# A masked attention kernel with 536 instead of 544 token places in its short path

## Chip, cores and metric

One core of one Trainium2 chip runs the whole program. The metric is the device time of one execution in microseconds. Everything is float32.

## The reference, cut to what matters

Eight sequences (B = 8) of T = 1024 tokens with D = 512 features go through one attention layer with eight heads and a residual. Queries, keys and values are the same projection `q`. The mask holds 0 or 1 for each token.

```python
def _L0_cond_ref(x, mask, Wq, Wo):          # x: (8, 512, 1024)
    xt = jnp.transpose(x, (0, 2, 1))
    q = xt @ Wq.T
    qh = q.reshape(B, T, NH, dk).transpose(0, 2, 1, 3)     # NH = 8, dk = 64
    scores = scale * jnp.einsum('bhqd,bhkd->bhqk', qh, qh)
    cmask = mask[:, None, None, :]
    rmask = mask[:, None, :, None]
    logits = (scores * cmask + (1.0 - cmask) * NEG) * rmask
    attn = jax.nn.softmax(logits, axis=-1)
    ctx = jnp.einsum('bhqk,bhkd->bhqd', attn, qh)
    out = ctx.transpose(0, 2, 1, 3).reshape(B, T, D) @ Wo.T
    return jnp.transpose(out, (0, 2, 1))
x = x + _L0_cond_ref(x, cond_2048, Wq, Wo)
```

A masked key gets weight zero. A masked query has all its logits at zero, so its attention is the plain mean over all 1024 tokens. Both follow from the mask alone: only the kept tokens (mask 1) need scores, and all masked queries of a batch share one context, the mean. The mask is drawn with a chance of 0.5063 for each token, so about half of the tokens are kept.

## The kernel before

The kernel packs the kept tokens of each batch into a fixed number of places NK, and the last place, NK - 1, stands for the mean. `early` (L1008) ranks the tokens of all masks, and a value that the program reads, the largest number of kept tokens in any batch (with 2T times over 1 added if a mask isn't 0 or 1), chooses a path at L1438 to L1445: `late(SHORT)` below 544, `late(LONG)` below 576, and otherwise a kernel over all tokens. `fit_to(n)` (L330) sets NK = n, KH = n / 2 and END = n - 512. Places are handled in NC = 5 chunks: four of 128 (LP = 512 places) and a last one of END, 32 in the path before.

A *pair* is two heads of one batch, that is 128 features; there are 32 pairs, four for each batch, taken in order. The loop at L1324 runs each pair through five steps c = 0 to 4. At each step TensorE gets, in a hand-written order:

- `scores(pair, c)` (L651): the scores of chunk c against all NK places, in two halves of KH columns, for two heads and two half chunks, as 64x64 matmuls on the four quarters of the array (L662; L676 for the last chunk). ScalarE turns them into exponentials (L685).
- at c = 0 and 1 `project` (L529) of the next pair: 64x64 matmuls over KH columns, the upper half with one more column for the mean (L542). `take_queries` (L554) then copies the two halves into `qT` (L558 on ScalarE, L559 on VectorE), fills `qT` behind place NK up to W = 640 places with copies of the last END columns (L560), and keeps the mean (L565).
- `weigh` (L697): values times exponentials, KH columns each, 64x64 again (L709).
- at c = 2 `turn_values` (L567): 64x64 transposes of the next pair's `qT` to `v` (L579, L588); then squares, lengths and biases for it.
- between them, by the plan of `plan` (L1179), work for other batches: gathering kept tokens (`gather`, L467, on POOL's queue), transposing them into `xc` (`collect`, L480), output products of finished batches (`output`, L822, whose results POOL's queue stores to `od` in DRAM at L846), `fetch` (L942: rows of `od` gathered and added to rows of x, also on POOL's queue), and `finish_blocks` (L909: VectorE transposes of finished rows into `whole`, stored by SP's queue).

`invert` (L779) sends the reciprocal sums through DRAM and back by SP's queue (`row`, `rb`); `contexts` (L808) multiplies them into the context `cT`, and copies the mean into its last column (L812). For the last batch `begin_output` and `end_output` (L856, L872) make the output product in two parts, and `fetch_last` and `finish_tokens` finish it.

Each engine's queue runs in order. So on VectorE the copies of `qT` stand behind whatever was put before them, `finish_blocks` and `contexts` included.

The output product of the last chunk is only END tokens wide. `output` therefore lays `parts = 128 // END` pieces of the 512 features side by side on the 128 partitions, and stores each with a DMA of its own.

Of the kernel before, what the change touches and what calls it, by code (L numbers as in the profile page):

```python
# [10 lines left out]
F32 = mybir.dt.float32  # L11
I32 = mybir.dt.int32
AF = mybir.ActivationFunctionType
ALU = mybir.AluOpType
# [5 lines left out]
NEG = -1e30  # L20
BIG = 3.0e38
Q = 32
SHORT = 544
LONG = 576
TINY = 1e-26

# [279 lines left out]
def attention_of_kept_tokens(ctx, tc, x, mask, wq, wo, out, ident, wqT, woT, verdict, flag):  # L306


    nc = tc.nc
    B, D, T = x.shape  # L310
    P = 128
    DK = D // NH
    SCALE = 1.0 / math.sqrt(DK)
    ND = D // P
# [8 lines left out]
    LP = LAST * P  # L323
    W = NC * P
    assert LP < SHORT < LONG == LP + DK and DK == P // 2
    NK = KH = END = 0
    sizes, places = [], []
    heads = [slice(h * DK, (h + 1) * DK) for h in range(2)]

    def fit_to(n):  # L330
        nonlocal NK, KH, END
        NK, KH, END = n, n // 2, n - LP
        assert DK % END == 0
        sizes[:] = [P] * LAST + [END]
        places[:] = [slice(END + c * P, END + (c + 1) * P) for c in range(LAST)] + [slice(0, END)]

    sb = ctx.enter_context(tc.tile_pool(name="fsb", bufs=2))
# [23 lines left out]
    def bank(name, tag="t"):  # L361
        return ps.tile([P, NB], F32, tag=tag, name=name, bufs=2)
# [141 lines left out]
    qTs, qms, vs, tops, biases, shares = {}, {}, {}, {}, {}, {}  # L504
# [2 lines left out]

    def place_queries(pair):
        b, pr = pair
        qTs[pair] = sb.tile([P, W], F32, tag="qT", name=f"qT_{b}_{pr}", bufs=2)  # L510
        pqs[pair] = [bank(f"pq_{b}_{pr}_{hf}") for hf in range(2)]

    def project_first(pair):

        b, pr = pair
        place_queries(pair)
        for hf in range(2):
            n = KH + hf
            for d in range(ND):
                nc.tensor.matmul(  # L520
                    pqs[pair][hf][:, :n],
                    wqT[:, d, pr * P : (pr + 1) * P],
                    xcs[b][:, d, hf * KH : hf * KH + n],
                    start=(d == 0),
                    stop=(d == ND - 1),
                )
        take_queries(pair)

    def project(pair, cross):  # L529


        b, pr = pair
        if not cross:
            place_queries(pair)
        for d in range(ND):
            for r in range(2):
                rows = slice(r * DK, (r + 1) * DK)
                hf = r ^ cross
                n = KH + hf
                for h in range(2):  # L540
                    at = pr * P + h * DK
                    mm = nc.tensor.matmul(  # L542
                        pqs[pair][hf][heads[h], :n],
                        wqT[rows, d, at : at + DK],
                        xcs[b][rows, d, hf * KH : hf * KH + n],
                        start=(not cross and d == 0),
                        stop=(cross == 1 and d == ND - 1),
                    )
                    if cross:
                        pass_gate(mm)  # L550
        if cross:
            take_queries(pair)

    def take_queries(pair):  # L554
        b, pr = pair
        qT = qTs[pair]
        lo, hi = pqs.pop(pair)
        note(nc.scalar.copy(qT[:, :KH], lo[:, :KH]))  # L558
        nc.vector.tensor_copy(qT[:, KH:NK], hi[:, :KH])  # L559
        nc.vector.tensor_copy(  # L560
            qT[:, NK:W].rearrange("p (r k) -> p r k", k=END),
            hi[:, KH - END : KH].unsqueeze(1).to_broadcast([P, (W - NK) // END, END]),
        )
        qms[pair] = sb.tile([P, 1], F32, tag="qm", name=f"qm_{b}_{pr}", bufs=4)
        nc.vector.tensor_copy(qms[pair], hi[:, KH : KH + 1])  # L565
# [68 lines left out]
    es, rbs, cTs, avs, begun = {}, {}, {}, {}, set()  # L634
# [3 lines left out]
    def note(read):  # L638
        reader[0] = reader[0] or read.ins.name
# [89 lines left out]
        weigh(pair, c - 1, cross)  # L729

    def place_contexts(pair):
        cTs[pair] = sb.tile([P, NK], F32, tag="cT", name="cT_%d_%d" % pair, bufs=2 * ND)
        return cTs[pair]

    def end_values(pair):
        cT = place_contexts(pair)
        for hf, av in enumerate(avs.pop(pair)):
            read = nc.scalar.copy(cT[:, hf * KH : (hf + 1) * KH], av[:, :KH])  # L738
        note(read)

    def end_values_last(pair):

        cT = place_contexts(pair)
        for hf, av in enumerate(avs.pop(pair)):
            cols = slice(hf * KH, (hf + 1) * KH)
            nc.vector.tensor_tensor(cT[:, cols], av[:, :KH], rbs[pair][:, cols], ALU.mult)
        nc.vector.tensor_copy(cT[:, NK - 1 : NK], qms.pop(pair))

    def spread(pair, inv):

# [48 lines left out]
    def sum_last(pair):  # L799

        rb = rbs[pair]
        end = rb[:, LP : LP + DK]
        nc.vector.tensor_tensor(end, end, rb[:, LP + DK : W], ALU.add)
        nc.vector.tensor_tensor(lowest, lowest, end, ALU.min)
        nc.vector.tensor_scalar(end, end, TINY, None, ALU.max)
        nc.vector.reciprocal(end, end)

    def contexts(pair):  # L808
        sum_last(pair)
        cT, rb = cTs[pair], rbs.pop(pair)  # L810
        nc.vector.tensor_tensor(cT, cT, rb[:, :NK], ALU.mult)
        nc.vector.tensor_copy(cT[:, NK - 1 : NK], qms.pop(pair))  # L812


    ods, gs, wholes, pos = {}, {}, {}, {}
# [1 line left out]
    def place_outputs(b):  # L817
        if b not in ods:
            ods[b] = dr.tile([NK, D], F32, tag="od", name=f"od_{b}")
        return ods[b]  # L820

    def output(b, i, k, of=2):  # L822

        n = sizes[i]
        parts = P // n
        w = D // parts
        if k == 0:
            pos[b, i] = sb.tile([P, D], F32, tag="oc", name=f"oc_{b}_{i}", bufs=NC)
        oc = pos[b, i]
        cols = slice(k * w // of, (k + 1) * w // of)  # L830
        po = bank(f"po_{b}_{i}_{k}")
        for pr in range(ND):
            for j in range(parts):
                nc.tensor.matmul(  # L834
                    po[j * n : (j + 1) * n, cols],
                    cTs[b, pr][:, i * P : i * P + n],
                    woT[:, pr, j * w + cols.start : j * w + cols.stop],
                    start=(pr == 0),
                    stop=(pr == ND - 1),
                )  # L840
        note(nc.scalar.copy(oc[:, cols], po[:, cols]))  # L841
        if k + 1 < of:
            return
        od = place_outputs(b)
        for j in range(parts):
            nc.gpsimd.dma_start(od[places[i], j * w : (j + 1) * w], oc[j * n : (j + 1) * n, :w])  # L846

    partials = {}

    def plain(pr):  # L850
        return woT[:, pr, :].rearrange("p (a d f) -> p d a f", a=A, d=ND)

    def as_plain(t):
        return t.rearrange("p (d a f) -> p d a f", a=A, d=ND)

    def begin_output(b, i):  # L856

        n = sizes[i]
        po = bank(f"pa_{b}_{i}")
        for pr in range(ND - 1):  # L860
            nc.tensor.matmul(  # L861
                as_plain(po[:n, :]),
                cTs[b, pr][:, i * P : i * P + n],
                plain(pr),
                start=(pr == 0),
                stop=(pr == ND - 2),
            )
        pa = sb.tile([P, D], F32, tag="xin", name=f"pa_{b}_{i}", bufs=NC)
        note(nc.scalar.copy(pa[:n, :], po[:n, :]))
        partials[i] = pa  # L870

    def end_output(b, i, tag):  # L872
        n = sizes[i]
        od = place_outputs(b)
        po = bank(f"po_{b}_{i}", tag)
        nc.tensor.matmul(
            as_plain(po[:n, :]),
            cTs[b, ND - 1][:, i * P : i * P + n],
            plain(ND - 1),
            start=True,  # L880
            stop=True,
        )
        oc = sb.tile([P, D], F32, tag="oc", name=f"oc_{b}_{i}", bufs=NC)
        nc.vector.tensor_tensor(oc[:n, :], po[:n, :], partials[i][:n, :], ALU.add)
        nc.sync.dma_start(od[places[i], :], oc[:n, :])

    def place_blocks():

# [290 lines left out]
    def plan():  # L1179
# [61 lines left out]
        for b in range(B - 1):  # L1241
            nxt = b + 1
            if b < B - 3:
                for i in range(LAST - 1):
                    put(nxt, i + 1, 3, output, b, i, 0, rank=6)
                    put(nxt, i + 1, 4, output, b, i, 1, rank=6)
# [47 lines left out]
    def late(n):  # L1294
# [63 lines left out]
        begin_output(B - 1, LAST)  # L1358
        sum_last(last)
        end_values_last(last)  # L1360
        for j, i in enumerate((0, LAST, *range(1, LAST))):
            end_output(B - 1, i, ("t", "av")[j % 2])
# [46 lines left out]
def kernel(  # L1409
# [22 lines left out]
    with ExitStack() as pools:  # L1432
# [5 lines left out]
        fit = nc.values_load(verdict[0:1, 0:1], min_val=0, max_val=2 * T)  # L1438
        with tc.If(fit < SHORT) as short:
            with tc.manual_schedule():  # L1440
                late(SHORT)
        with short.Else():
# [35 lines left out]
```

## Time and profile before

| | |
|---|---|
| median of 3 runs | 677.13 us (675.56 to 678.43) |
| the profiled execution | 679.92 us |
| its span, first to last instruction | 677.9 us |
| mean granted TensorE clock | 0.963 |
| share of the span busy: PE, DVE, ACT, POOL | 92%, 53%, 53%, 27% |

The profile names engines PE (TensorE matmuls), PEld (its weight loads), DVE (VectorE), ACT (ScalarE), POOL (GpSimd) and SP; a q behind the name is the engine's sequencer, which waits and issues DMAs. L662 is line 662 of the kernel before. A group's row gives line, engine, operation, output and inputs by the program's names, shapes and count, then busy time in us and the mean of one in ns, then the engine's idle time just before these instructions and what ended it. The chain is followed back from the last instruction, at each step to what released it. Matmuls overlap in the rows, so one matmul's length is not the pace at which they run; the pace is read from starts, or from a piece of the chain divided by its count. Each matmul of the code between different tiles is recorded as two instructions, each transpose of `xc` as one.

### The profile page before, as it was taken

What the parts mean: (1) busy time and instruction counts of PE and PEld (TensorE: products, weight loads), DVE (VectorE), ACT (ScalarE), POOL (GpSimd) and SP (SyncE); (2) the same over time, 40 slices, a digit from 0 to 9 for tenths busy, and PEclk for the clock granted to TensorE, in tenths of its full rate; (3) what the DMA queues carried; (4) which work ended last, traced back from release to release, by engine and by line L of the source; (5) the groups of instructions that cost most, each with busy time, mean ns of one, the idle gap of its engine ahead of it and who ended that gap; (6) DMA issues with size and microseconds to landing.
All of it is one profiled execution on the core that took longest, in us unless ns stands there. A gap on an engine that the chain in (4) does not pass through costs nothing.

```text
span 677.9 us, 21834 instructions
## 1 busy us (share of the span) xinstructions
PE 621.4 (92%) x9056; PEld 413.2 (61%) x9056; DVE 362.0 (53%) x1113; ACT 360.5 (53%) x1010; POOL 184.1 (27%) x203
## 2 busy tenths in 40 slices
PE   6578989999999979999999999999999999998953
PEld 5345657677666656667666666676666655554422
DVE  6325885654564555555664566457645535234252
ACT  5127667656655645556656665656655445544300
POOL 4600221100134212341224304331334207006240
PEclk9688999999999989999999999999999999998985
DMA  8533663533366865696769777785857468744666
GB/s 277 170 122 98 197 192 89 165 97 113 103 197 141 215 185 154 205 252 164 198 227 247 169 187 247 195 196 150 233 135 144 130 212 154 211 146 78 128 197 190
DMA packets 98544, 117.10 MB, mean 173 GB/s; under 512 B 11785, under 2 KB 65625, under 8 KB 98426
## 3 DMA queue, kind: packets, MB, share of 16 engines
q1 hardware_dynamic: 77976, 75.71, 37.4%
q0 software_dynamic: 16224, 37.71, 24.4%
q10 hardware_dynamic: 4226, 2.10, 1.1%
q8 instruction: 75, 1.23, 0.8%
q14 instruction: 43, 0.35, 0.2%
HBM read 72.81 MB, written 42.67 MB: 170 GB/s over the span
## 4 chain that ended last, share of the span: by engine, by line
PE 76%; DMA 8%; DVE 7%; ACT 3%; SPq 2%; issue 2%; POOL 1%; DVEq 0%; ACTq 0%; POOLq 0%
PE s L662 17%; PE av L709 17%; PE pq L542 15%; PE po L834 15%; PE v L579 3%; DMA x<-in_x_dram 2%; PE pa L861 2%; PE xc L485 2%; DVE len L601 1%; ACT e L685 1%; DVE xc L488 1%; PE top L615 1%; PE s L676 1%; DMA rb<-row 1%; DMA g<-od,origin 1%
## 5 line engine op out<-in xcount | busy, mean ns | idle before, releaser
L685 ACT ACTIVATE e<-s,bias 128x544 f32<-128x544 f32 x256 | 180.3, 709 | 89.1 <-PE s L662 88.7
L709 PE MATMUL av<-e,v 64*64 64x272 f32 x2048 | 162.5, 398 | 7.9 <-ACT el L685 4.3
L662 PE MATMUL s<-qT 64*64 64x272 f32 x2048 | 155.8, 399 | 0.0
L542 PE MATMUL pq<-xc,wqT 64*64 64x272 f32 (+1 forms) x1984 | 127.5, 390 | 0.2 <-DVE xc L488 0.2
L709 PEld LDWEIGHTS av<-e,v 64*64 64x64 f32 x2048 | 85.5, 134 | 52.6 <-ACT cT L738 8.5
L834 PE MATMUL po<-woT,cT 128*128 128x256 f32 (+2 forms) x624 | 114.7, 363 | 0.0
L662 PEld LDWEIGHTS s<-qT 64*64 64x64 f32 x2048 | 82.3, 134 | 36.2 <-issue 6.9
L542 PEld LDWEIGHTS pq<-xc,wqT 64*64 64x64 f32 x1984 | 79.2, 134 | 37.5 <-issue 0.8
L943 POOL DMA_INDIRECT g<-od,origin x48 | 75.8, 1578 | 84.8 <-DMA g<-xd 60.5
L834 PEld LDWEIGHTS po<-woT,cT 128*128 128x128 f32 (+1 forms) x624 | 79.2, 164 | 28.8 <-issue 15.1
L846 POOL DMA_DIRECT2D od<-oc x56 | 31.3, 562 | 202.6 <-ACT oc L841 200.4
L472 POOL DMA_INDIRECT xin<-xd,source x40 | 39.8, 995 | 130.8 <-DMA row<-rt 71.8
L488 DVE COPY xc<-xc 128x512 f32<-128x512 f32 (+1 forms) x37 | 22.0, 613 | 61.4 <-PE xc L485 61.4
L559 DVE COPY qT<-pq 128x272 f32<-128x272 f32 x32 | 14.1, 439 | 70.2 <-PE pq L542 65.2
L841 ACT COPY oc<-po 128x256 f32<-128x256 f32 (+2 forms) x57 | 21.7, 382 | 55.8 <-PE po L834 55.8
L685 ACT ACTIVATION_READ_ACCUMULATOR e<-s,bias 128x1 f32 x256 | 50.2, 196 | 0.0
L588 DVE COPY v<-v 128x320 f32<-128x320 f32 x64 | 28.3, 483 | 34.3 <-PE v L579 34.3
L913 DVE STREAM_TRANSPOSE whole<-g 128x512 f32<-128x512 f32 x56 | 37.4, 687 | 13.8 <-DMA g<-od,origin 9.1
L601 DVE TENSOR_REDUCE len<-sq 128x10 f32<-128x640 f32 x32 | 26.1, 814 | 30.5 <-ACT sq L595 30.4
L738 ACT COPY cT<-av 128x272 f32<-128x272 f32 x62 | 21.1, 389 | 37.6 <-PE av L709 37.5
L425 ACT ACTIVATE junka<-x 128x512 f32<-128x512 f32 x64 | 40.2, 628 | 0.7
L462 DVE TENSOR_SCALAR_CACHE_REDUCE junk<-rank,key 128x1024 f32<-128x1024 f32 (+4 forms) x40 | 39.8, 996 | 0.0
(156 smaller groups left out, 633.4 us busy)
## 6 DMA issues: line engine op xcount, KB each, us to landing
xd<-xt SPq DMA_DIRECT2D x120, 128.0 KB
x<-in_x_dram SPq DMA_DIRECT2D x56, 256.0 KB
g<-xd SPq DMA_DIRECT2D x48, 256.0 KB
out_dram<-whole SPq DMA_DIRECT2D x20, 512.0 KB
rb<-row SPq DMA_DIRECT2D x60, 160.0 KB
od<-oc POOLq DMA_DIRECT2D x28, 256.0 KB
out_dram<-whole SPq DMA_DIRECT2D x16, 256.0 KB
rank<-ranks SPq DMA_DIRECT2D x7, 512.0 KB
```

The lines of the kernel that those rows point to most:

```text
L425: nc.scalar.activation(junk, xs[b][r][:, d, :], AF.Copy, accum_out=xbars[b][:, d, r : r + 1])
L462: nc.vector.tensor_scalar(junk[:, :n], rank[:, i * P :], key[:, col], 0.0, ALU.is_le, ALU.add, accum_out=found[:, col])
L472: nc.gpsimd.indirect_dma_start(out=xin[:n, :], out_offset=None, in_=rows_of_x[b], in_offset=bass.IndirectOffsetOnAxis(ap=searches[b][2][:n ...
L542: mm = nc.tensor.matmul(pqs[pair][hf][heads[h], :n], wqT[rows, d, at : at + DK], xcs[b][rows, d, hf * KH : hf * KH + n], start=(not cross ...
L601: nc.vector.tensor_reduce(lengths, sq.rearrange("p c (h d) -> p (c h) d", h=2), axis=AX.X, op=ALU.add,)
L662: nc.tensor.matmul(s[h][to, hf, :KH], qT[heads[h], at : at + DK], qT[heads[h], hf * KH : (hf + 1) * KH], start=True, stop=True,)
L685: act = nc.scalar.activation(e[:, h], of[h], AF.Exp, bias=biases[pair][:, c : c + 1], scale=SCALE, accum_out=acc[:, h, c : c + 1],)
L709: mm = nc.tensor.matmul(avs[pair][hf][heads[h], :KH], v[rows, c, heads[h]], e[rows, h, hf, :] if c < LAST else e[rows, h, :], start=(c == ...
L834: nc.tensor.matmul(po[j * n : (j + 1) * n, cols], cTs[b, pr][:, i * P : i * P + n], woT[:, pr, j * w + cols.start : j * w + cols.stop], st ...
L846: nc.gpsimd.dma_start(od[places[i], j * w : (j + 1) * w], oc[j * n : (j + 1) * n, :w])
L913: nc.vector.transpose(whole.rearrange("p (d a) n -> p a d n", a=A)[:, :, :, i * Q : (i + 1) * Q], gs.pop((b, i)).rearrange("p (a d f) -> p ...
L943: nc.gpsimd.indirect_dma_start(out=gs[b, i], out_offset=None, in_=ods[b], in_offset=bass.IndirectOffsetOnAxis(ap=origin[:, b, i : i + 1] i ...
```

## The change

The short path has 536 places instead of 544, so KH is 268 instead of 272 and END is 24 instead of 32. The largest number of kept tokens must now be under 536 for this path; between 536 and 575 the path of 576 places is taken. Because 24 does not divide 32, 64 or 128, several places treat the last chunk as `max(Q, END)` = 32 wide: the fill behind the keys copies blocks of 32 (four blocks, 128 columns, instead of three, 96, so `qT` has 664 columns), `cT` stays 544 wide with the mean written into its last nine columns, and the output product of the last chunk is computed 32 wide but stored 24 wide. In the path of 576 places END is 64 as before.

```diff
-SHORT = 544
+SHORT = 536
...
     def fit_to(n):
         nonlocal NK, KH, END
         NK, KH, END = n, n // 2, n - LP
-        assert DK % END == 0
+        assert max(Q, END) in (Q, DK)
...
     def place_queries(pair):
         b, pr = pair
-        qTs[pair] = sb.tile([P, W], F32, tag="qT", name=f"qT_{b}_{pr}", bufs=2)
+        span = max(Q, END)
+        n = NK + -(-(W - NK) // span) * span
+        qTs[pair] = sb.tile([P, n], F32, tag="qT", name=f"qT_{b}_{pr}", bufs=2)
...
         nc.vector.tensor_copy(qT[:, KH:NK], hi[:, :KH])
+        span = max(Q, END)
+        again = qT[:, NK:].rearrange("p (r k) -> p r k", k=span)
         nc.vector.tensor_copy(
-            qT[:, NK:W].rearrange("p (r k) -> p r k", k=END),
-            hi[:, KH - END : KH].unsqueeze(1).to_broadcast([P, (W - NK) // END, END]),
+            again, hi[:, KH - span : KH].unsqueeze(1).to_broadcast([P, again.shape[1], span])
         )
...
     def place_contexts(pair):
-        cTs[pair] = sb.tile([P, NK], F32, tag="cT", name="cT_%d_%d" % pair, bufs=2 * ND)
+        cTs[pair] = sb.tile([P, LP + max(Q, END)], F32, tag="cT", name="cT_%d_%d" % pair, bufs=2 * ND)
...
+    def mean_last(pair):
+        cT = cTs[pair]
+        n = cT.shape[1] - NK + 1
+        nc.vector.tensor_copy(cT[:, NK - 1 :], qms.pop(pair).to_broadcast([P, n]))
...
     def contexts(pair):
         sum_last(pair)
         cT, rb = cTs[pair], rbs.pop(pair)
-        nc.vector.tensor_tensor(cT, cT, rb[:, :NK], ALU.mult)
-        nc.vector.tensor_copy(cT[:, NK - 1 : NK], qms.pop(pair))
+        nc.vector.tensor_tensor(cT[:, :NK], cT[:, :NK], rb[:, :NK], ALU.mult)
+        mean_last(pair)
...
     def output(b, i, k, of=2):
-        n = sizes[i]
+        n = max(Q, sizes[i])
...
         for j in range(parts):
-            nc.gpsimd.dma_start(od[places[i], j * w : (j + 1) * w], oc[j * n : (j + 1) * n, :w])
+            nc.gpsimd.dma_start(od[places[i], j * w : (j + 1) * w], oc[j * n : j * n + sizes[i], :w])
...
     def end_output(b, i, tag):
-        n = sizes[i]
+        n = max(Q, sizes[i])
...
-        nc.sync.dma_start(od[places[i], :], oc[:n, :])
+        nc.sync.dma_start(od[places[i], :], oc[: sizes[i], :])
```

`end_values_last` calls `mean_last` in place of its own copy, and `begin_output` takes `n` as `end_output` does.

More of the change, by code (lines that the diff above doesn't have):

```diff
@@ L810, in contexts @@
         cT, rb = cTs[pair], rbs.pop(pair)
-        nc.vector.tensor_tensor(cT, cT, rb[:, :NK], ALU.mult)
-        nc.vector.tensor_copy(cT[:, NK - 1 : NK], qms.pop(pair))
+        nc.vector.tensor_tensor(cT[:, :NK], cT[:, :NK], rb[:, :NK], ALU.mult)
+        mean_last(pair)
     ods, gs, wholes, pos = {}, {}, {}, {}
@@ L872, in end_output @@
     def end_output(b, i, tag):
-        n = sizes[i]
+        n = max(Q, sizes[i])
         od = place_outputs(b)
```

## The prediction

> **What bounds the kernel now.** I read the page's busy shares first, then its chain of work that ended last, then the busy time by stretches.
>
> ```profile
> span 677.9 us, 21834 instructions
> PE 621.4 (92%) x9056; PEld 413.2 (61%) x9056; DVE 362.0 (53%) x1113; ACT 360.5 (53%) x1010; POOL 184.1 (27%) x203
> PE 76%; DMA 8%; DVE 7%; ACT 3%; SPq 2%; issue 2%; POOL 1%; DVEq 0%; ACTq 0%; POOLq 0%
> ...
> 255.00:545.00 290.00, 288.52 (x4491) 198.34 (x4484) 167.95 (x519) 170.88 (x487) 89.98 (x88) 1.00 0.71 191
> ```
>
> TensorE is busy for 92% of the span and holds 76% of the chain; VectorE and ScalarE are at 53%. In the stretch from 255 to 545 us (columns: length, then busy time of PE, weight loads, DVE, ACT, POOL, the granted clock, the DMA share, GB/s) PE is idle for 1.5 us of 290, at a granted clock of 1.00, while the DMA engines are 71% busy. A busy PE need not be a PE at its peak, so the question is what sets its pace. The chain in order of time, without a window and then in two windows (start, length, what), tells it, and its head gives the shares by line.
>
> ```profile
> by line: PE s L662 17.2%; PE av L709 16.6%; PE pq L542 15.4%; PE po L834 15.3%; PE v L579 2.7%; DMA x<-in_x_dram 2.4%; PE pa L861 2.0%; PE xc L485 2.0%; issue 1.5%; DVE len L601 1.3%; ACT e L685 1.2%; DVE xc L488 1.2%; PE top L615 1.2%; PE
> ...
> 31.40 5.17 PE pq L520 x16
> ...
> 316.10 0.44 PE xc L485 x4
> 316.54 1.08 PE s L662 x16
> 317.62 1.84 PE pq L542 x32
> 319.45 0.92 PE av L709 x16
> ...
> 343.69 0.58 PE v L579 x30
> ...
> 350.20 1.73 PE po L834 x8
> ```
>
> The 64x64 matmuls of scores (s), values (av) and projections (pq) run four at a time, one on each quarter of the array; I call four of them a step. pq x32 is eight steps in 1.84 us, 230 ns each; av x16 is four in 0.92, 230 ns. A full-array matmul of 256 columns takes 1.73/8 = 216 ns (po), one of 128 columns 0.44/4 = 110 ns (xc). From 128 to 256 columns that is 106 ns for 128 columns, 0.83 ns a column; on this line 272 columns would be 216 + 16 x 0.83 = 229 ns, which is what the steps take. So a step's time is its columns times 0.83 ns plus about 3 ns. One more check that columns and nothing else set it: the half of pq that carries the mean has 273 columns, an odd number, and its rows show no penalty.
>
> ```profile
> L542 PE MATMUL pq<-xc,wqT 64*64 64x273 f32 x992 | 125.1, 391 | 0.0
> L542 PE MATMUL pq<-xc,wqT 64*64 64x272 f32 x992 | 124.7, 390 | 0.2 <-DVE xc L488 0.2
> L709 PE MATMUL av<-e,v 64*64 64x272 f32 x2048 | 162.5, 398 | 7.9 <-ACT el L685 4.3 <-DVE v L588 1.8 <-ACT e L685 0.9
> ```
>
> (Shape, count, busy us, mean ns of one, idle time before.) These xc columns also start at row pitches of 545 words, so at all sorts of addresses, and run at the same pace; the new pitches (268, 537) should be no worse.
>
> **The change, part by part.** *Four columns fewer in each step of s, av and pq.* 4 x 0.83 = 3.3 ns of 229, 1.45%. Recorded instructions: 2048 and 256 for s (L662, L676), 2048 and 256 for av, 1984 for pq, and 16 full-array ones at L520 that are a step each: 6592/4 + 16 = 1664 steps, so 5.5 us if every one were on the path. Not all are: before 30 us, from 72 to 97 and from 215 to 250 us the chain runs through DMAs and small VectorE work. I take the chain's own share: (17.2 + 16.6 + 15.4)% of 677.9 = 333.5 us, of which 1.45% is 4.84 us. L676 has 64 steps, at most 0.2 us; I take half, 0.1. L520 has 5.17 x 1.45% = 0.07. Together 5.0 us. A page of the Trainium skill speaks against this term; it stands with the rivals.
>
> *Exponentials.* Each of the 256 large ones loses 8 elements, each of the 64 small ones 4.
>
> ```profile
> L685 ACT ACTIVATE e<-s,bias 128x544 f32<-128x544 f32 x256 | 180.3, 709 | 89.1 <-PE s L662 88.7
> L685 ACT ACTIVATE el<-s,bias 128x272 f32<-128x272 f32 x64 | 30.6, 483 | 14.1 <-PE s L676 13.9
> L811 DVE TENSOR_TENSOR cT<-cT,rb 128x544 f32<-128x544 f32 x31 | 22.5, 727 | 1.1
> L559 DVE COPY qT<-pq 128x272 f32<-128x272 f32 x32 | 14.1, 439 | 70.2 <-PE pq L542 65.2 <-PE pq L520 5.0
> L560 DVE COPY qT<-pq 128x96 f32<-128x96 f32 x32 | 7.9, 247 | 0.0
> L812 DVE COPY cT<-qm 128x1 f32<-128x1 f32 x31 | 4.8, 154 | 1.1
> L488 DVE COPY xc<-xc 128x128 f32<-128x128 f32 x7 | 2.0, 280 | 0.0
> ```
>
> (709 - 483)/272 = 0.83 ns an element, so 6.6 ns of 709, 0.9%. ScalarE mostly waits for scores (88.7 us), so this counts only in its 1.2% of the chain, 8.1 us: 0.08 us.
>
> *VectorE, for each pair of heads.* The fill behind the keys (L560) grows from 96 columns to four blocks of 32, 128 columns: between 247 ns and the 280 ns of the 128x128 copy out of PSUM; I take 280, +33 ns, or 33/32 = 1.03 ns a column. The copy of the upper half (L559) loses 4 columns, -4 ns; L811 loses 8, -8; the mean is written into 9 columns instead of 1 (L812): between 154 and 247 ns, I take +8. Net +29 ns. What hides it: TensorE needs qT for its transposes (v, L579) a step of scores and one of values later.
>
> ```profile
> 305.82 0.25 DVE L560 COPY qT<-pq 128x96 f32<-128x96 f32 x1
> 305.98 0.15 DVE L565 COPY qm<-pq 128x1 f32<-128x1 f32 x1
> 306.16 1.09 PE L709 MATMUL av<-e,v 64*64 64x272 f32 x16
> 306.85 0.48 PEld L579 LDWEIGHTS v<-ident,qT 64*64 64x64 f32 x13
> PE v L579 <- DVE qm L565: 4.6, 2, 4.0
> ```
>
> (Timeline: start, length; last row a wait: total, times, longest.) qm is done at 306.13 and the first weight load of the transposes comes at 306.85, a cover of 0.7 us for the 29 ns. PE sat idle for qm only twice in 32; with two more places that are close I charge four, 0.12 us. With the cover gone at all 32 it would be 0.9 us.
>
> *The last chunk of 24 tokens.* Its output product stays 32 wide (8 columns hold the mean), so its time stays. Its transposes into xc go from 32 to 24 columns, 32 instructions: nothing to 32 x 8 x 0.83 = 0.2 us gained, I take 0. Its copy has 96 columns for 128, about 33 ns each on 8 batches, behind DVE's idle time. The gather of 24 rows and the four stores of 24 rows stand in POOL's queue; POOL is 27% busy, and its waits are mostly for outputs. I take 0; the other end is a rival below.
>
> Sum against the profiled execution: it took 679.92 us (span 677.9, so 2.0 around it), 0.4% above the median of the three runs shown, 677.13. -5.0 - 0.08 + 0.12 = -5.0 us gives 674.9 for such an execution and, with the same 5.0, **672.1** for the median.
>
> **The rivals.** *The DMAs set the pace of the middle (675).* There PE has almost no idle time, but VectorE already waits there for gathered rows, and it stands in order.
>
> ```profile
> 466.91 0.71 DVE L913 STREAM_TRANSPOSE whole<-g 128x512 f32<-128x512 f32 x1 [0.65 <-DMA g<-od,origin]
> ...
> 470.45 0.70 PEld L579 LDWEIGHTS v<-ident,qT 64*64 64x64 f32 x40 [0.36 <-issue]
> ...
> DVE whole L913 <- DMA g<-od,origin: 2.9, 3, 1.3
> ```
>
> At 466.9 the transposes of finished rows wait 0.65 us for a gather; contexts and the copies of qT queue behind, and TensorE's v comes 0.36 us late. Against it: between 255 and 612 us there are three such waits, 2.9 us in all, and a pair (about 18 us of that stretch, 16 pairs in all) has 1664/32 = 52 steps and gets only 52 x 3.3 = 0.17 us shorter, against a cover of 0.7. If the DMAs did hold the 16 pairs of that stretch to their time, 16 x 0.17 = 2.8 us would be lost: 674.9 for the median.
>
> *A late gather stops VectorE at more batches (slower, 680).* Once, at 246.5 us, PE stands for 4.0 us (the wait for qm above): rows gathered from od come late, `whole` waits 4.7 us at the head of VectorE's queue, and contexts and qT with it.
>
> ```profile
> 246.94 0.71 DVE L913 STREAM_TRANSPOSE whole<-g 128x512 f32<-128x512 f32 x1 [4.66 <-DMA g<-od,block_origin]
> 247.58 0.18 DVE L803 TENSOR_TENSOR rb<-rb 128x64 f32<-128x64 f32 x1
> POOL g L943 <- DMA od<-oc: 12.2, 5, 3.5
> ```
>
> POOL's gathers of od wait for its stores (12.2 us, five times). If the stores of 24 rows land later, or the sooner arrival of TensorE meets the same late rows, two more such stops cost 8.0 - 5.0 = +3 us: 680. It decides once a batch's rows come more than the 0.7 us of cover later. For it: POOL's and SP's queues are in order, and a small shift lines up differently. Against it: the stores get smaller, and DMA-led stretches shift as a whole with the TensorE work ahead of them.
>
> *Issue, not columns, sets a step (677).* Then four columns are worth nothing and the extra 29 ns stay: 677.2. Against it stand the three lengths on one line, and the 30 transposes of 64 columns in 0.58 us, 19 ns each, where a step's matmuls come every 57 ns. The Trainium skill (TensorE: Matmul & The Clock Gate, "Wait — 56ns, not 53.3ns?") gives about 62 ns of sequencer time for each matmul when hardware decoding is off, as the bound for short ones; by it a step would be 248 ns and the change worth nothing. The trace disagrees, with 57 and 19 ns.
>
> *The masks don't fit (699).* The path is taken if the largest number of kept tokens is under 536. Counting the reference's mask as its default seed makes it gives 505, 529, 523, 514, 519, 519, 533 and 521, so 533 fits. The trace by itself says only that it is under 544. If not, the path of 288 columns runs: 16 x 0.83 x 1664 = +22 us.
>
> **How the numbers follow.** TensorE's columns: 0.80, with its own range 670.2 to 674. DMAs hold the middle: 0.10. Issue: 0.03. More stops: 0.05. Masks: 0.02. Runs of this kernel differ by 2.9 us, and a measurement of it can tell about 0.5% (3.4 us) from no change, so faster begins under 673.7. Of the first case about 0.74 lies there, and a little of the second: 0.76 faster. Slower than 680.5: half of the stops and the masks, and some scatter, 0.05. The rest, 0.19, is the same. The range goes from 669.8 (all 1664 steps on the path, and scatter) to 675.9, past the second case.
>
> **What would show it.** Steps of 225 to 226 ns: pq x32 in 1.81, av x16 in 0.90; e at 702 ns, L560's copy at 280; PE idle between 255 and 545 us still under 3 us; the stop near 246 us once, near 4 us long. I am wrong if the steps stay at 229 ns, if `whole` waits for gathers in more batches, or if PE's idle time grows by what its steps save.

## The result, and the profile after

| | before | after |
|---|---|---|
| median of 12 runs each | 677.27 us (675.56 to 680.17) | 674.07 us (672.21 to 681.66) |
| ratio after / before, 95% interval | | 0.9957 (0.9936 to 0.9977) |
| the profiled execution | 679.92 us | 673.16 us |
| its span, mean granted clock | 677.9 us, 0.963 | 671.1 us, 0.970 |

The kernel became faster by 2.9 us by the ratio (1.6 to 4.3), 3.2 by the medians. That is 0.43%, just short of the 0.5% that the prediction took as the bound of what can be told. The two profiled executions differ by more, 6.8 us, and the first task is to say which part of that belongs to the change. (The median and the interval rest on all 12 runs of each kernel; each profile shows only one of them.)

The busy shares, the chain's shares, and the stretch from 255 to 545 us of the kernel after (length, then busy time of PE, weight loads, DVE, ACT, POOL, clock, DMA share, GB/s):

```profile
span 671.1 us, 21834 instructions
PE 613.0 (91%) x9056; PEld 410.6 (61%) x9056; DVE 363.3 (54%) x1113; ACT 358.3 (53%) x1010; POOL 185.2 (28%) x203
PE 73%; DMA 9%; DVE 7%; ACT 3%; SPq 3%; issue 2%; POOL 1%; DVEq 0%; ACTq 0%; POOLq 0%
...
255.00:545.00 290.00, 287.99 (x4500) 198.59 (x4494) 169.67 (x520) 170.06 (x486) 91.10 (x88) 1.00 0.73 194
```

The middle is as full as it was: PE idle for 2.0 us of 290 (1.5 before), nine more matmuls recorded in the same time, and the DMA engines at 73% instead of 71%. The chain of the kernel after in order of time, around 330 us (start, length, what), shows the steps:

```profile
330.16 1.06 PE s L665 x16
331.23 1.81 PE pq L544 x32
333.04 0.90 PE av L712 x16
333.94 0.90 PE s L665 x16
```

Eight steps of pq take 1.81 us, 226 ns each, where 1.84 stood; four of av take 0.90 instead of 0.92. Then the groups of instructions by shape (shape, count, busy us, mean ns of one, idle time before):

```profile
L544 PE MATMUL pq<-xc,wqT 64*64 64x269 f32 x992 | 123.5, 388 | 0.0
...
L688 ACT ACTIVATE e<-s,bias 128x536 f32<-128x536 f32 x256 | 178.6, 702 | 85.5 <-PE s L665 85.2
...
L819 DVE TENSOR_TENSOR cT<-cT,rb 128x536 f32<-128x536 f32 x31 | 22.2, 717 | 1.1
L561 DVE COPY qT<-pq 128x268 f32<-128x268 f32 x32 | 13.9, 435 | 66.5 <-PE pq L544 61.6 <-PE pq L522 4.9
L564 DVE COPY qT<-pq 128x128 f32<-128x128 f32 x32 | 9.0, 280 | 0.0
...
L755 DVE COPY cT<-qm 128x9 f32<-128x9 f32 x32 | 5.9, 184 | 1.1
```

Exponentials at 702 ns, the fill behind the keys at 280, the upper half's copy 4 ns shorter. Since the profiled executions disagree with the medians, the span has to be cut into pieces. I take the start of the first last-chunk score matmul of each pair (L676 before, L679 after) and the time from each to the next: the length of a pair. Two such starts in the chain of the kernel before, and the same two in the kernel after, give 18.20 and 18.04 us for the first pair of the fifth batch:

```profile
330.14 0.62 PE s L676 x8
348.34 0.62 PE s L676 x8
```

```profile
325.57 0.61 PE s L679 x8
343.61 0.61 PE s L679 x8
```

| pair | before | after | difference |
|---|---|---|---|
| from the start of the program to the first pair's mark | 57.84 | 57.21 | -0.62 |
| second of the second batch | 17.67 | 17.51 | -0.16 |
| third of the second batch | 18.69 | 18.53 | -0.16 |
| fourth of the second batch | 17.79 | 17.65 | -0.14 |
| fourth of the third batch (the stop near 246 us) | 24.26 | 22.60 | -1.66 |
| second of the seventh batch | 17.86 | 18.38 | +0.52 |
| fourth of the eighth batch | 23.08 | 21.61 | -1.47 |
| from the last pair to the end | 43.31 | 44.26 | +0.95 |
| the 28 pairs not disturbed, with the three of the second batch above | | | -4.47 |
| the span | 677.87 | 671.11 | -6.76 |

24 of the 31 pairs measured in this way are shorter by 0.14 to 0.17 us, and the 28 outside the three disturbed ones sum to -4.5 us. If the first pair and the three disturbed ones gain 0.16 us each as well, columns give -5.1 us in all; that is an estimate. The start of the program is 0.62 us shorter, but most of this isn't columns: the first projections, the first matmuls that lose four columns, already begin 0.42 us sooner than the 31.40 us of the kernel before. (In the executions of the experiments below this stretch takes 56.9 to 59.3 us, in no order of size.)

```profile
30.98 5.07 PE pq L522 x16
```

The three disturbed pairs and the end sum to -1.7 (-1.66 + 0.52 - 1.47 + 0.95), of which columns would be 0.5; the rest turns on clock and stops. First the stop, in the kernel after: the waits (total, times, longest), and VectorE's and the weight loads' timeline.

```profile
PE v L582 <- DVE qm L568: 4.0, 2, 3.4
...
243.87 0.71 DVE L921 STREAM_TRANSPOSE whole<-g 128x512 f32<-128x512 f32 x1 [3.87 <-DMA g<-od,block_origin]
...
246.63 0.43 DVE L561 COPY qT<-pq 128x268 f32<-128x268 f32 x1
246.97 0.28 DVE L564 COPY qT<-pq 128x128 f32<-128x128 f32 x1
...
247.44 0.70 PEld L582 LDWEIGHTS v<-ident,qT 64*64 64x64 f32 x40 [3.84 <-issue]
```

`whole` waits 3.87 us for gathered rows, the copies of qT stand behind it, and the transposes to v begin at 247.44 after 3.84 us without a weight load. The stop is where it was, 0.8 us shorter (`whole` waited 4.66 us in the kernel before). Then the windows after the stop, first in the kernel after, then in the kernel before, with the stretch near 618 us as well:

```profile
245.10:248.50 3.40, 1.03 (x48) 1.00 (x52) 3.30 (x9) 0.00 (x0) 0.00 (x0) 1.00 0.97 257
248.50:251.90 3.40, 3.40 (x30) 2.08 (x22) 0.74 (x2) 2.11 (x5) 0.00 (x0) 0.50 0.73 155
```

```profile
249.00:255.80 6.80, 5.29 (x73) 3.47 (x74) 3.37 (x8) 2.10 (x5) 0.00 (x0) 0.50 0.71 196
617.60:621.00 3.40, 2.89 (x28) 2.38 (x32) 0.45 (x4) 0.75 (x2) 2.79 (x3) 0.51 0.57 79
```

After the stop TensorE was granted half its clock: for 3.4 us in the execution after, for 6.8 in the one before. A stretch at half speed costs half of the time for which PE was busy in it, up to 1.7 us for 3.4. PE was busy for 5.29 us at half clock before and for 3.40 after, so by this estimate the longer stretch cost 0.9 us; with the 0.8 of the shorter stop that is about the 1.66 of the fourth pair. Near 618 us the execution before had one more such stretch, with PE busy for 2.89 us (1.4 us of cost), and the one after none: its matmuls of the reciprocals (first row before, second after) took 2.40 and 1.31 us.

```profile
618.11 2.40 PE L756 MATMUL rb<-ident,ris 128*64 128x128 f32 x20 [2.73 <-DVE ris L776]
```

```profile
611.84 1.31 PE L764 MATMUL rb<-ident,ris 128*64 128x128 f32 x20 [2.73 <-DVE ris L784]
```

Both follow the same wait of 2.73 us, and of the changed kernel's other executions shown below one has that pair at 21.61 us (`third536`) and one at 23.23 (`again536`): this stretch comes and goes with the same program. Of the 6.8 us, then, 4.5 are seen in pairs that shrink evenly and 5.1 are columns by the estimate above; the other 1.7 are taken as luck of this pair of executions. (The Trainium skill, in TensorE: Matmul & The Clock Gate, "What's actually happening", names two rates, half and full, and a window of about 3.4 us that runs freely. The rows agree with the two rates, at 0.50 and 1.00, and with the window, in stretches of 3.4 and 6.8 us; that it runs freely they do not show.)

### The profile page after: what moved, and what is told of

It is laid out like the page before. It is cut to its first block, busy times and chain, and to the rows that moved or that the text cites. A ratio compares the mean times of both kernels' runs of the same rounds, so it can differ in the third digit from the quotient of the medians.

```text
span 671.1 us, 21834 instructions
## 1 busy us (share of the span) xinstructions
PE 613.0 (91%) x9056; PEld 410.6 (61%) x9056; DVE 363.3 (54%) x1113; ACT 358.3 (53%) x1010; POOL 185.2 (28%) x203
## 4 chain that ended last, share of the span: by engine, by line
PE 73%; DMA 9%; DVE 7%; ACT 3%; SPq 3%; issue 2%; POOL 1%; DVEq 0%; ACTq 0%; POOLq 0%
PE s L665 16%; PE av L712 16%; PE po L842 15%; PE pq L544 15%; DMA x<-in_x_dram 3%; PE v L582 2%; PE pa L869 2%; PE xc L485 2%; PE s L679 1%; DVE junk L462 1%; PE top L618 1%; DMA rank<-ranks 1%; DVE len L604 1%; ACT e L688 1%; DMA g<-od,origin 1%
## 5 line engine op out<-in xcount | busy, mean ns | idle before, releaser
L688 ACT ACTIVATE e<-s,bias 128x536 f32<-128x536 f32 x256 | 178.6, 702 | 85.5 <-PE s L665 85.2
L712 PE MATMUL av<-e,v 64*64 64x268 f32 x2048 | 160.8, 395 | 8.1 <-ACT el L688 4.3
L665 PE MATMUL s<-qT 64*64 64x268 f32 x2048 | 153.6, 394 | 0.0
L544 PE MATMUL pq<-xc,wqT 64*64 64x268 f32 (+1 forms) x1984 | 125.8, 387 | 0.2 <-DVE xc L488 0.2
L951 POOL DMA_INDIRECT g<-od,origin x48 | 75.5, 1574 | 84.1 <-DMA g<-xd 59.3
L561 DVE COPY qT<-pq 128x268 f32<-128x268 f32 x32 | 13.9, 435 | 66.5 <-PE pq L544 61.6
L741 ACT COPY cT<-av 128x268 f32<-128x268 f32 x62 | 20.8, 385 | 36.8 <-PE av L712 36.8
```

The lines of the kernel that those rows point to most:

```text
L544: mm = nc.tensor.matmul(pqs[pair][hf][heads[h], :n], wqT[rows, d, at : at + DK], xcs[b][rows, d, hf * KH : hf * KH + n], start=(not cross ...
L665: nc.tensor.matmul(s[h][to, hf, :KH], qT[heads[h], at : at + DK], qT[heads[h], hf * KH : (hf + 1) * KH], start=True, stop=True,)
L688: act = nc.scalar.activation(e[:, h], of[h], AF.Exp, bias=biases[pair][:, c : c + 1], scale=SCALE, accum_out=acc[:, h, c : c + 1],)
L712: mm = nc.tensor.matmul(avs[pair][hf][heads[h], :KH], v[rows, c, heads[h]], e[rows, h, hf, :] if c < LAST else e[rows, h, :], start=(c == ...
L951: nc.gpsimd.indirect_dma_start(out=gs[b, i], out_offset=None, in_=ods[b], in_offset=bass.IndirectOffsetOnAxis(ap=origin[:, b, i : i + 1] i ...
```

## The experiments

The runs below were made on two chips, in three sets: the first and the third set on one chip, the second on the other. There the kernel before takes 693 to 694 us, not 677; the place where the result was measured is called the first place, and it isn't recorded which chip that was. So each kernel is compared only with the runs of the kernel before in its own set. My theory: the columns of the 64x64 steps on TensorE's path give about -5 us, in proportion, and nothing else of the change matters. Rivals: the smaller stores and gathers of the last chunk change the time; odd or awkward column counts do; the stop near 246 us is what the change acts on.

**The changed kernel again, and its DMAs put back (first set).** `cap536` is the changed kernel unaltered. `rows32` keeps 268 columns in all matmuls, but gathers and stores the last chunk as 32 rows, with `od` 544 rows long:

```diff
-        places[:] = [slice(END + c * P, END + (c + 1) * P) for c in range(LAST)] + [slice(0, END)]
+        edge = max(Q, END)
+        places[:] = [slice(edge + c * P, edge + (c + 1) * P) for c in range(LAST)] + [slice(0, edge)]
...
     def gather(b, i):
-        n = sizes[i]
+        n = max(Q, sizes[i])
...
-            nc.gpsimd.dma_start(od[places[i], j * w : (j + 1) * w], oc[j * n : j * n + sizes[i], :w])
+            nc.gpsimd.dma_start(od[places[i], j * w : (j + 1) * w], oc[j * n : (j + 1) * n, :w])
...
-        nc.sync.dma_start(od[places[i], :], oc[: sizes[i], :])
+        nc.sync.dma_start(od[places[i], :], oc[:n, :])
...
```

Expected of `cap536`:

> The changed kernel unaltered, for a second profile and more times. Theory 'columns': each step of four 64x64 matmuls is 3.3 ns shorter, so every pair of the middle is again 0.15 to 0.16 us shorter than before (17.70 instead of 17.86 us for the second pair of a batch), and the median is 5 us under the kernel before. Rival 'scatter': the pairs are shorter all the same, but two or three places that wait for DMAs (near 244 us, near 502 us, the end) differ by 1 to 2 us from one execution to the next, so that the difference of the medians comes out anywhere from 2 to 6 us. Rival 'small stores': the places that wait for DMAs are longer than before each time, and the difference stays near 3 us.

Expected of `rows32`:

> The changed kernel with 536 token places in all matmuls, but the last chunk gathered from x as 32 rows and stored to the output rows as 32, in 544 rows as before (the eight extra rows repeat the mean). Theory 'columns' and rival 'scatter': within 1 us of the changed kernel. Rival 'small stores' (24 rows land later and give 2 of the 5 us back): 2 us faster than the changed kernel, and the waits of VectorE for gathered rows shorter.

| kernel, first set | median (lowest to highest) | ratio to before (95%) |
|---|---|---|
| before | 693.38 (688.63 to 699.14) | |
| cap536 | 687.70 (684.23 to 689.75) | 0.9893 (0.9855 to 0.9931) |
| rows32 | 688.81 (685.98 to 692.18) | 0.9906 (0.9870 to 0.9942) |
| cap540 | 691.65 (690.44 to 695.14) | 0.9988 (0.9966 to 1.0011) |
| long576 | 711.95 (708.65 to 713.60) | 1.0257 (1.0220 to 1.0295) |

The gain is there with 32 rows too; the two intervals cover each other almost entirely. By the medians `rows32` is 1.1 us slower than `cap536`, not 2 us faster, and VectorE's waits for gathered rows are not shorter (8.4 and 4.0 us for the two kinds of gather, against 7.8 and 3.3). The size of the DMAs for the last chunk neither cost nor gave anything that can be seen, though intervals of 0.37% to each side (2.6 us) don't by themselves exclude 2 us.

**Columns in proportion (the same set).** `cap540` has 270 columns, `long576` sets the bound so low that the masks go to the path of 576 places, with 288 columns:

```diff
-SHORT = 536
+SHORT = 540
```

```diff
-SHORT = 536
+SHORT = 520
```

Expected of `cap540`:

> 540 places: 270 columns, a last chunk of 28. Theory 'columns': half of the effect, each middle pair 0.08 us shorter than before (17.78 us for the second pair of a batch), the median 2.5 us under the kernel before, exponentials at 706 ns. Rival 'small stores': 28 rows are no multiple of 8, so the DMA side is no better than with 24 and the median only 0.5 us under the kernel before.

Expected of `long576`:

> The short path's bound set below the largest number of kept tokens, so that the path of 576 places runs: 288 columns, a last chunk of 64. Theory 'columns': 32 places more than before at 0.155/8 us a place and pair, each middle pair 0.62 us longer (18.5 us for the second pair of a batch), in all 32 x 0.62 = 20 us, 697 us; the steps 242 ns. Rival 'something other than columns sets the step': 677 to 680.

The chain of `long576` by time, around 331 us:

```profile
330.97 1.95 PE pq L544 x32
332.92 0.97 PE av L712 x16
333.89 0.97 PE s L665 x16
```

Steps of 243 ns (0.97/4, 1.95/8), and a whole that is 17.8 us slower (15.3 to 20.5), a little under what was expected. The median of `cap540` is only 1.7 us under before; by the ratio it is 0.8 (from 2.4 less to 0.8 more), which includes no change and the 0.5 us of the rival and leaves out the 2.5 expected from columns. So the total at 540 places doesn't bear the theory out, and why it falls short isn't shown (`rows32` speaks against the rows of the last chunk). The lengths of pairs say more than the totals, since the fourth pair of the second batch is disturbed in none of the profiled executions:

| places | length of that pair, us | us for each place from the row above |
|---|---|---|
| 534 (below) | 17.62 | |
| 536 | 17.65 | 0.015 |
| 540 | 17.73 | 0.020 |
| 544 | 17.79 | 0.015 |
| 576 | 18.38 | 0.018 |

536 gave 17.65 and 544 gave 17.79 in every profiled execution, those of the first place among them. From 534 to 576 the slope is 0.76/42 = 0.018 us a place; 52 steps of half a column each at 0.83 ns would be 0.022, a little more; the difference isn't explained. The fill is 128 columns wide at 536 and 540 places, 96 at 544 and 64 at 576, and leaves no step in this table. So columns set the length of a pair, in proportion, over five sizes.

**Where 536 and 544 differ by chance: the stop near 246 us (second set).** In `cap544`, the changed text with 544 places, VectorE's `whole` waits in the same place, but shorter:

```profile
250.89 0.71 DVE L921 STREAM_TRANSPOSE whole<-g 128x512 f32<-128x512 f32 x1 [2.21 <-DMA g<-od,block_origin]
```

The pair that holds it took 24.26 us in the kernel before, 22.60 in the one after, 19.30 in `cap544`, 20.36 in `cap536` and 18.38 in `long576`. At 544 places alone it cost 6.5 us (24.26 - 17.79) and 1.5 us, in `long576` nothing (18.38 is that kernel's undisturbed length). One program on one chip had 20.36 and 22.07 us (`cap536`, and `third536` below). So the stop, with the half clock behind it, varies by as much as a good part of what the whole change gives. To take it away, the last block of the first batch is put later in the plan, from step 1 to step 4 of that pair, in both sizes (`later544`, `later536`):

```diff
                 ends = [(nxt + 1, *at) for at in ends]
+                if b == 0:
+                    ends[NT - 1] = (2, 3, 4)
```

Expected of `cap544`:

> The changed program text with 544 places, which lays out and issues what the kernel before does: a second profile of it on the same chip as the next three. All theories: the time of the kernel before, undisturbed pairs of the middle 17.80 us (the last pair of a batch). Rival 'scatter': the pair of the stop near 246 us (24.3 us in the kernel before) takes anything from 18 to 25 us.

Expected of `again536`, the changed kernel once more:

> The changed kernel unaltered, beside the same on this chip. Theory 'columns': 5 us under the kernel before, 17.65 us for the undisturbed last pair of a batch. Rival 'the stops eat it': those pairs are 0.15 us shorter, but the sum over the places that wait for DMAs (the third and fourth pair of the third batch, the third pair of the first, the end) is 2 us longer than with 544, and the medians differ by 3 us.

Expected of `later544`:

> 544 places, and the last of the first batch's transposes of finished rows moved three steps later, from the second to the last step of the fourth pair of the third batch, so that it no longer stands ahead of the copies of qT while its gather is under way. If this gather makes the stop: that pair takes 18 to 19 us instead of 22 to 24, the time is 3 to 5 us less than with 544 places and no move. If the row of reciprocals (rb) is late as well, it stays above 21 us.

Expected of `later536`:

> The same move with 536 places. Theory 'columns': 5 us less than the same move with 544 places, with less scatter than the two kernels without the move, and 3 to 5 us under the changed kernel. Rival 'the stops eat it': the difference of the two moved kernels is 5 us where that of the unmoved ones is 3.

| kernel, second set | median (lowest to highest) | ratio to before (95%) | that pair, us |
|---|---|---|---|
| before | 694.48 (689.82 to 698.83) | | |
| cap544 | 694.39 (690.27 to 698.59) | 1.0002 (0.9972 to 1.0032) | 19.30 |
| again536 | 690.42 (685.01 to 694.70) | 0.9929 (0.9896 to 0.9961) | 22.22 |
| later544 | 690.22 (687.65 to 693.07) | 0.9939 (0.9910 to 0.9969) | 17.79 |
| later536 | 687.37 (682.80 to 689.19) | 0.9879 (0.9827 to 0.9930) | 17.65 |

The changed text at 544 places issues what the kernel before does (a fill of 96 columns, the mean in one), so `cap544` compares a program with itself: the ratio of 1.0002, known to 0.3%, shows how fine such a comparison is. It doesn't test the wider fill and the mean in nine columns, which come only with a smaller size. The profiled execution of `again536` is the slowest of its 12 and that of `cap544` the fastest, so these two traces don't tell how much of the gain the stops eat. Moving one transpose is worth 4.2 us at 544 places by the medians, about as much as the change studied. In `later536` the transpose waits for nothing and the copies of qT are free:

```profile
249.79 0.67 DVE L921 STREAM_TRANSPOSE whole<-g 128x512 f32<-128x512 f32 x1
...
252.77 0.44 DVE L561 COPY qT<-pq 128x268 f32<-128x268 f32 x1 [0.17 <-PE pq L544]
```

The gain of the size is there with the stop and without: 544 to 536 is -4.0 us with it (694.39 to 690.42) and -2.9 without (690.22 to 687.37). So the stop is not what the change acts on.

**The same kernels against each other once more, and 534 places (third set, on the chip of the first).** `third536`, `third_later544` and `third_later536` are the kernels of the sets above under new names. `third_later534` has the moved transpose too, and goes as near to the masks' largest count, 533, as it can: 267 columns, an odd number.

```diff
-SHORT = 536
+SHORT = 534
```

Expected of `third536`:

> The changed kernel unaltered once more. Theory 'columns and the clock': the undisturbed last pairs of a batch take 17.65 us again, the difference from the kernel before is 5 us at equal mean clock, and the rest of the scatter goes with the mean granted clock of each execution: each 3.4 us at half clock costs about 1.7 us and lowers the mean by 0.0025. In the profile the extra length of a pair stands beside a stretch of half clock (near 85 to 90 us, near 250 us, near 620 us). Rival 'the stops eat it': 3 us at equal clock.

Expected of `third_later544`:

> 544 places and the moved transposes: 3 to 4 us under the kernel before, no stretch of half clock near 250 us, the fourth pair of the third batch 17.79 us.

Expected of `third_later536`:

> 536 places and the moved transposes: 5 us under the last one, 8 to 9 us under the kernel before, that pair 17.65 us. If the columns' gain were eaten by the stop near 246 us, this difference would be larger than that between the kernels without the move; if not, the same 5 us.

Expected of `third_later534`:

> 534 places, 267 columns, a last chunk of 22, and the moved transposes. Theory 'columns': undisturbed pairs 0.04 us shorter again (17.61 us), 1.2 us under 536 places. If an odd number of columns (267, and so halves that start at odd words) costs something, it is slower than 536 places.

| kernel, third set | median (lowest to highest) | ratio to before (95%) |
|---|---|---|
| before | 693.58 (688.53 to 699.61) | |
| third536 | 689.08 (687.75 to 694.85) | 0.9947 (0.9919 to 0.9975) |
| third_later544 | 692.09 (690.60 to 693.70) | 0.9978 (0.9952 to 1.0004) |
| third_later536 | 685.00 (682.99 to 688.18) | 0.9885 (0.9848 to 0.9921) |
| third_later534 | 685.15 (682.42 to 686.71) | 0.9868 (0.9831 to 0.9906) |

Here the moved transpose gives 1.5 us at 544 places, less than expected, and 4.1 at 536, and the size gives 4.5 with the stop (693.58 to 689.08) and 7.1 without. The single differences scatter by some 2 us around their middle, though each is made of 6 to 29 runs. The clock explains a part of the scatter, but less than expected: a straight line through the runs of this set other than its slowest one, with the same slope for each kernel, falls by 1.0 us for each 0.0025 of mean clock, not 1.7, and at equal clock leaves 4.4 us between `third536` and before. The odd count does no harm: 534 and 536 places are the same within the scatter, and by pairs 534 is shorter in proportion. 536 places with the moved transpose have the lowest median in both sets of runs, 1.2% under before by the ratios (0.9879 and 0.9885); 534 places are not shown to be better.

## Why the prediction was right, and where its size was off

**The columns: right.** Steps went to 225 to 226 ns (pq x32 in 1.81, av x16 in 0.90), the 28 undisturbed pairs shrank evenly and give -4.5 us, or -5.1 for all 32 by the estimate above, against the -5.0 of the sum. Shown by the lengths of pairs at five sizes from 534 to 576 places. The totals of runs bear it out less closely: -2.9 to -7.1 us for eight places.

**VectorE: right that it is hidden, one term too small.** The fill takes 280 ns as taken, L561 and L819 lose 4 and 10 ns for the forecast 4 and 8. The mean in nine columns takes 184 ns, 30 more than the one column had, not 8 more; it is inside the bounds given. In all that is 49 ns more for each pair instead of 29, and the cover of 0.7 us holds: TensorE still waited for qm twice, not four times as the sum took it.

**The small DMAs: nothing speaks against the 0 that was taken.** `rows32` shows no difference within its interval, and POOL's gathers wait about as long for the stores as they did (12.2 us before):

```profile
POOL g L951 <- DMA od<-oc: 11.9, 5, 3.2
```

**The rivals.** That DMAs hold the middle falls with the pairs there, each 0.15 us shorter; that issue sets a step, with 226 and 243 ns at two other widths; that the masks don't fit, with the 536-wide rows. More stops did not come: between 250 and 606 us the waits of `whole` are what they were,

```profile
DVE whole L921 <- DMA g<-od,origin: 2.9, 3, 1.5
```

and one new gap of 0.39 us near 502 us is all. (The second pair of the seventh batch, 0.52 us longer, holds that gap.)

**What was off: the size at the first place, and the certainty about it.** The time came out 2 us above the forecast, at 674.07, inside the range; but the measured step of 0.43% lies on the other side of the 0.5% from the case that was given 0.76. The weak step is in how the numbers follow: "Runs of this kernel differ by 2.9 us". Three runs of the kernel before show that; 12 runs of the two kernels show spreads of 4.6 and 9.5 us. The sum took everything but columns as fixed from execution to execution, and had no term for the change of the stop from one execution to the next, which cost from 1.5 to 6.5 us at 544 and 536 places, nor for the stretches at half clock, up to 1.7 us each. The runs after bear the clock out: the three with the highest mean clock (0.970, 0.968, 0.967) took 673.16, 672.21 and 672.94, the one with the lowest (0.954) 681.66. With that scatter, a gain of 5 us by the path and a measured 2.9 (1.6 to 4.3) are not the same number, yet the four comparisons of unaltered 536 places with the kernel before (-3.2, -5.7, -4.1 and -4.5 us by medians) have -4.4 as their mean (2.9 to 7.4 us less by the ratios).

**What stays open.** Whether the 3.2 us at the first place are chance or something of that place: only one trace of each kernel is at hand from it, and the experiments ran where the kernel before takes 693 to 694 us. The interval there excludes 5.0, which speaks against chance alone; the -4.1 of `again536` and the scatter of the single differences speak for it. Two places may give a part of the columns' gain back. From the last pair to the end the seven profiled executions with 536 places take 44.0 to 46.1 us and the four with 544 take 43.2 to 44.7, 0.9 us less by the means; but the one with 534 takes 43.7. And on the two chips of the experiments the half-clock stretch near 85 to 90 us stands in six of the seven profiled executions with 536 or 534 places and in one of the five with more. Both counts are too small to show it, and no run tried it.

## What to carry to other kernels

Price a narrower matmul as columns x ns per column x the steps on the path, and check it on a stage that nothing disturbs: the length of one such stage, the same to 0.01 us in every execution, told 534 places from 536, and 540 from 544, where the medians of runs could not. When the expected gain is about as large as the spread of the runs, say so in the forecast: look in the profile for stops that hang on a DMA and for granted clock under 1.00, and count them as terms that change from run to run. An instruction that waits for a DMA at the head of an in-order queue is worth moving: a later place in the plan took away a stop of up to 6 us.

## What the runs showed of the hardware that was not expected

**Half clock after a half-idle window.** TensorE need not be idle to lose its clock. `again536` has such a stretch near 88 us: first the window ahead of it, then the stretch, then the piece of the chain that ran in it.

```profile
84.30:87.70 3.40, 1.92 (x13) 0.57 (x16) 0.30 (x2) 0.85 (x3) 3.10 (x6) 1.00 0.86 221
87.70:91.10 3.40, 3.40 (x32) 1.95 (x35) 0.00 (x0) 1.21 (x4) 0.79 (x2) 0.50 0.75 255
```

```profile
88.67 3.10 PE pq L544 x31
```

PE was busy for 1.92 us of the 3.40 ahead of it, and for 1.03 in the kernel after ahead of 248.5; eight steps of pq, most of them in the stretch, then took 3.10 us instead of 1.81. Busy time alone doesn't decide it: from 610.27 to 613.68 us in the kernel after, a window in step with its stretch at half clock, PE was busy for only 1.84 us, and the clock stayed at 1.00 there and behind it. The same Trainium skill section speaks of at least one idle window ahead of half rate; these rows have windows that are only partly idle. Such a stretch isn't tied to 536 places: `third_later544` has one too (the row below), `third_later536` none there.

```profile
85.60:89.00 3.40, 3.31 (x28) 1.73 (x31) 0.00 (x0) 2.17 (x6) 1.65 (x4) 0.51 0.88 241
```

**Late matmuls with no visible wait.** Ahead of that stretch, in the third pair of the first batch, matmuls come late with nothing that the trace names; PE of `again536`:

```profile
83.72 0.68 PE L665 MATMUL s<-qT 64*64 64x268 f32 x3 [0.29 <-issue]
85.19 1.87 PE L665 MATMUL s<-qT 64*64 64x268 f32 x8 [0.79 <-issue]
```

That pair took 19.00 us before and 18.77 after at the first place, and 22.0 to 25.3 on the two chips of the experiments, at any number of places. POOL was busy for 3.10 of 3.40 us then, and the DMA engines 86%; whether either causes it was not tried.

**The place of measurement differs by more than the change.** The same program took 677 us where the result was measured, and 693 to 694 on the two chips of the experiments; whether the chip or something around it makes this was not told apart. The places that can be named: that third pair (3 to 6 us), and the first pair of each middle batch, 19.0 instead of 18.0 us, where ScalarE's copies of av into the contexts (L741) come late in `cap536`:

```profile
194.40 0.68 PE L712 MATMUL av<-e,v 64*64 64x268 f32 x8 [0.80 <-ACT cT L741]
```

The fourth pairs of the second, fourth, fifth and sixth batch are the same to 0.01 us in all of them at the same number of places, so in these pairs neither the clock nor the pace of the array differs.
